# A four-layer attention network on one core: block-end copies, a norm in three parts, gates and a bias moved

## The chip, the cores and the metric

The kernel runs on one core of a Trainium2 chip. A core has five engines that work side by side, each through its own list of instructions: TensorE (PE, matrix products; its weight loads are listed as PEld), VectorE (DVE), ScalarE (ACT), GpSimd (POOL) and SyncE (SP), which here only issues transfers. The products land in PSUM[...]; DVE and ACT carry them from there to SBUF. The metric is the time of the whole program on the device in microseconds (us); lower is better.

## The reference, cut to what matters

Input is `x`, two images of 64 x 64 positions with 128 channels. Four residual layers follow each other: attention with relative positions, a triangle product, attention with an expert layer, attention with an expert layer. The change touches the first two.

```python
def _gn(v, G=32, eps=1e-5):                      # group norm over the positions of one image
    g = v.reshape(B_, H_, W_, G, C_ // G)
    return ((g - mean(g)) / sqrt(var(g) + eps)).reshape(v.shape)

# layer 0: x = x + L0(_gn(x))
scores = einsum('bnqd,bnkd->bnqk', q, k) * scale + pos     # 2 images, 4 heads, 4096 x 4096
out = einsum('bnqk,bnkd->bnqd', softmax(scores), v)

# layer 1: x = x + L1(_gn(x))
xn = layer_norm(x, norm_a, norm_b)
left = (xn @ Wl + bl) * sigmoid(xn @ Wlg + blg)
right = (xn @ Wr + br) * sigmoid(xn @ Wrg + brg)
out_gate = sigmoid(xn @ Wog + bog)
out = einsum('bkjd,bkid->bijd', left, right) / n           # the triangle product
out = layer_norm(out, on_a, on_b) * out_gate
return out @ Wo + bo
```

## The kernel before

All of `x` stays in SBUF as 64 blocks of 128 positions x 128 channels. Everything is float32.

**Layer 0** (`l0_bounded`) works in eight units: image, pair of heads, half of the queries. A unit has four blocks of 512 queries (`qb`), a block 32 steps of 128 keys (`k`). In a step PE makes the scores of two heads (L588, `l0sc`), ACT takes the exponential (L596, `l0es`), DVE multiplies with the position factor `ew` (L597), and the product with the values is made two steps later by `values()` (L546, `l0o`). `waiting` holds the two steps in between. When a block's last key has been multiplied, `values()` copies the sums out of PSUM, half on ACT (L555), half on DVE (L556), into `os`; `l0o` has one buffer, so the next block's first product waits for both copies. Then `l0_finish` adds the two halves of `os` (L705), transposes, divides and adds to `x`. In the text the multiply of a step stands before the call of `values()`.

Between the steps the text hands out small pieces of other work: `piece()` the next unit's queries, keys and position factors (`l0_prepare`) and `l0_finish`; `more()`, every fourth step, group statistics and, once image 0 is through (from half of layer 0 on), layer 1's norm of image 0 (`l1_first`).

**Layer 1** starts with the second image's norm, which can't start before layer 0 ends. `l1_rows` makes the group statistics and spreads them to rows (`gb`, L150), then for all eight groups of four blocks the group norm (L157, L158: DVE, 128 x 512), then for all 32 blocks the row statistics (L165, L166), then one chain for the reciprocal roots (`rstd`, L93 to L102, with a square root on ACT, L95), then 32 normalizations, even blocks on DVE (L169), odd ones on ACT (L428). `l1_turn` then transposes a group of four blocks on PE (L443) and brings it back through ACT with `norm_a` and `norm_b` (L444). `gates` makes the output gate of a group: a product (L897) and an eviction by ACT (L900); image 0's gates stand before image 1's norm, image 1's behind each turn. The sigmoid of the gates stands in the text among the projections (L947).

The projections (L925) take columns of `xT` with stride 64, so they need both images whole. 32 pairs follow each other: products on PE, bias on DVE (L933), sigmoid on ACT (L937), two multiplies on POOL (L939). Then comes the triangle product (L960), brought out by ACT (L967) into `tri`; beside it the text adds the bias `bo` to `x` on DVE (L974, sixteen times). `bo` itself is loaded at the start of layer 1 with the weights, by SP. Behind the triangle product SP loads the table for layer 2 (`kept`, L1040, 1792 KB), and DVE makes the statistics of `tri`.

What sets the order: the text gives each instruction its dependencies and its rank, and a planner fixes each engine's list when the program is built. An engine's list is not the text's order. In the trace, for example, the adds of L974 run from 2201.5 us on, before the projections, and the gates' sigmoids of L947 start at 2189.2 us.

Of the kernel before, what the change touches and what calls it, by code (L numbers as in the profile page):

```python
# [39 lines left out]
class Net:  # L40
# [356 lines left out]
    def l1_first(self, ps, xT, st, gb, na, nb):  # L397

        nc = self.nc
        for _ in self.l1_rows(ps, xT, 0, st, gb):  # L400
            yield
        for g in range(NC // 4):
            self.l1_turn(ps, xT, 0, g, na, nb)
            yield

    def l1_rows(self, ps, xT, b, st, gb):


        nc = self.nc
        self.group_rows(ps, gb, self.group_stats(ps, st, b))  # L410
        yield
        y = xT.rearrange("p (n c) -> p n c", c=C)
        mv = self.small.tile([P, NC, 2], F32, tag="l2mv", name=f"l1mv{b}", bufs=2)
        for g in range(NC // 4):
            blk = slice(4 * g, 4 * g + 4)
            self.group_norm(y[:, blk, :], b, g, gb)
            yield
        for n in range(0, NC, 2):
            self.row_stats(mv[:, n : n + 2, :], y[:, n : n + 2, :], f"l1{b}_{n}")
            yield  # L420
        r = self.small.tile([P, NC], F32, tag="l2r", name=f"l1r{b}", bufs=2)
        self.rstd(r, mv[:, :, 1], 1e-5, NC)
        m = self.small.tile([P, NC], F32, tag="l1m", name=f"l1m{b}", bufs=1)
        nc.vector.scalar_tensor_tensor(m, mv[:, :, 0], -1.0, r, ALU.mult, ALU.mult)
        yield
        for n in range(NC):
            if n % 2:
                nc.scalar.activation(  # L428
                    y[:, n, :], y[:, n, :], AF.Identity, bias=m[:, n : n + 1], scale=r[:, n : n + 1]
                )  # L430
            else:
                self.normalize(y[:, n, :], y[:, n, :], mv, r, n)
            if n % 4 == 3:
                yield

    def l1_turn(self, ps, xT, b, g, na, nb):
# [27 lines left out]
    def l0_bounded(self, xT, w, pe, gst, na, nb):  # L464
# [13 lines left out]
        nc, tc = self.nc, self.tc  # L478
        H2 = L // 2
        with (  # L480
# [91 lines left out]
            for i, unit in enumerate(units):  # L572
                ready(unit)
                qa, ew = made[unit]
                b, pair, half = unit
                ka = kas[pair]
                if i + 1 < len(units):
                    side.append(self.l0_prepare(ap, ps, units[i + 1], xT, wqk, pe, kas, made))
                for qb in range(4):
                    qs = slice(qb * 512, (qb + 1) * 512)  # L580
                    t = f"{b}_{pair}_{half}_{qb}"
                    for k in range(NC):
                        sc = ps.tile([P, 2, 512], F32, tag="sc", name=f"l0sc{t}_{k}")
                        for h in range(2):
                            rows = slice(64 * h, 64 * h + 64)
                            for c in range(2):
                                k0 = k * P + 64 * c
                                nc.tensor.matmul(  # L588
                                    sc[64 * c : 64 * c + 64, h, :],
                                    lhsT=ka[rows, k0 : k0 + 64],  # L590
                                    rhs=qa[rows, k // (NC // 2), qs],
                                    start=True,
                                    stop=True,
                                )
                        es = ap.tile([P, 2, 512], F32, tag="es", name=f"l0es{t}_{k}", bufs=3)
                        nc.scalar.activation(es, sc, AF.Exp)  # L596
                        nc.vector.tensor_tensor(es, es, ew[:, :, qs], ALU.mult)  # L597
                        if len(waiting) == 2:
                            values()
                        waiting.append((unit, qb, k, es))  # L600
                        if k % 2:
                            piece()
                        elif k % 4 == 2:
                            more()
# [236 lines left out]
    def layer1(self, xT, gst, na, nb, xp, kp):  # L841
# [3 lines left out]
        nc, tc, ins = self.nc, self.tc, self.ins  # L845
        GN = 16
        with ExitStack() as st:
            wp = st.enter_context(tc.tile_pool(reuse_waits="tile", name="l1w", bufs=1))
            sp = st.enter_context(tc.tile_pool(reuse_waits="tile", name="l1n", bufs=2))
            big = st.enter_context(tc.tile_pool(reuse_waits="tile", name="l1b", bufs=1))  # L850
            names = ("l", "r", "lg", "rg", "og")
            wcat = wp.tile([P, 5 * C], F32, tag="wcat", name="wcat")
            bcat = wp.tile([P, 4 * C], F32, tag="bcat", name="bcat")
            for i, n in enumerate(names):
                nc.sync.dma_start(out=wcat[:, i * C : (i + 1) * C], in_=ins[f"L1_conv_W{n}"])
                if i < 4:
# [10 lines left out]
                )  # L867
            )
            wo = self.load(wp, "wo", [P, C], ins["L1_conv_Wo"])
            bo = self.load(wp, "bo", [P, C], row_bcast(ins["L1_conv_bo"], C))  # L870

            def stats(src, tag):

# [14 lines left out]
                else:  # L888
                    self.normalize(rows, rows, mv, r, i)

            gate = big.tile([P, B, L], F32, tag="gate", name="l1gate")
            with tc.tile_pool(reuse_waits="tile", name="l1p", bufs=6, space=PSUM) as ps:

                def gates(b, g):
                    blk = slice(g * 512, (g + 1) * 512)
                    pg = ps.tile([P, 512], F32, tag="misc", name=f"l1pg{b}_{g}")
                    nc.tensor.matmul(  # L897
                        pg, lhsT=wcat[:, 4 * C :], rhs=xT[:, b, blk], start=True, stop=True
                    )
                    nc.scalar.activation(gate[:, b, blk], pg, AF.Identity, bias=bog)  # L900

                self.group_block(ps, gst[:, 1], 1, NC // 4 - 1)
                gb = sp.tile([P, 2 * C], F32, tag="gb", name="l1gb", bufs=1)
                rows = self.l1_rows(ps, xT[:, 1, :], 1, gst[:, 1], gb)
                next(rows)
                for g in range(NC // 4):
                    gates(0, g)
                for _ in rows:
                    pass
                for g in range(NC // 4):  # L910
                    self.l1_turn(ps, xT[:, 1, :], 1, g, na, nb)
                    gates(1, g)
            xnT = xT.rearrange("p b l -> p (b l)")
            gate = gate.rearrange("p b l -> p (b l)")


            lr = kp.tile([P, 2, C, S], F32, tag="k", name="lr")
            with (
                tc.tile_pool(reuse_waits="tile", name="l1t", bufs=3) as tp,
                tc.tile_pool(reuse_waits="tile", name="l1q", bufs=3, space=PSUM) as ps,  # L920
            ):
                for j in range(0, S, 2):
                    p1 = ps.tile([P, 2, 4 * C], F32, tag="lr", name=f"l1p1_{j}")
                    for k in range(2):
                        nc.tensor.matmul(  # L925
                            p1[:, k, :],
                            lhsT=xnT[:, j + k :: S],
                            rhs=wcat[:, : 4 * C],
                            start=True,
                            stop=True,  # L930
                        )
# [1279 lines left out]
```

## Time and profile before

| | |
|---|---|
| runs, median of 3 | 4906.94 us (4905.28 to 4908.01) |
| the profiled execution | 4914.85 us, its span 4913.0 us |
| TensorE's mean granted clock | 0.954 of full |
| busy: PE, DVE, ACT, POOL | 4556.6 (93%), 2937.1 (60%), 2666.8 (54%), 922.1 (19%) us |

The stretches of layer 1 in the same execution, busy microseconds of each engine in each stretch:

| stretch, us from the start | PE | DVE | ACT | POOL | clock | what runs |
|---|---|---|---|---|---|---|
| 2173 to 2183 | 6.01 | 3.57 | 3.57 | 0.00 | 0.50 | group statistics |
| 2183 to 2193 | 9.27 | 9.55 | 6.50 | 0.00 | 0.80 | group norm, gates of image 0 |
| 2193 to 2202 | 0.00 | 9.00 | 4.80 | 0.00 | 0.73 | row statistics |
| 2202 to 2208 | 0.00 | 6.00 | 0.23 | 0.00 | 0.50 | reciprocal roots, adds of `bo` |
| 2208 to 2242 | 21.82 | 9.54 | 21.28 | 0.00 | 0.56 | normalization, turns, gates of image 1 |
| 2242 to 2300 | 54.95 | 39.19 | 21.92 | 45.38 | 1.00 | projections |
| 2300 to 2319 | 17.82 | 0.00 | 14.96 | 0.47 | 0.83 | triangle product |
| 2319 to 2360 | 22.46 | 34.23 | 26.68 | 18.16 | 0.68 | norm of the product, gate |

In a line of a timeline the first number is the start in us, the second the time that it takes; then engine, line, operation, what is written and read, shapes, and how many were merged. In square brackets stands how long the engine had been idle and what ended that. In a line of the costliest groups, behind the bar, stand the busy time and the mean of one in ns, and behind the second bar the engine's idle time ahead of them and what ended most of it. A matrix product of the text is listed as two instructions.

### The profile page before, as it was taken

Reading aid. Unit: us, or ns where it says so; the run is one execution under the profiler, and the core shown is the slowest. Engines: PE = TensorE matmul, PEld = TensorE weight load, DVE = VectorE, ACT = ScalarE, POOL = GpSimd, SP = SyncE. Lnnn points to the kernel's source line nnn. Section 1 sums busy time; section 2 is a strip of 40 time slices with the busy share of each in tenths; the row PEclk is TensorE's granted clock in tenths of the full one; section 3 lists DMA queues with packets and bytes.
Section 4 is the critical chain, followed back from the end, with each engine's and each line's share of the span. In section 5 each row is a group of like instructions: output and inputs, shape, how many; then the busy total and the mean of one; then the engine's idle time right before and its main releaser. Section 6 shows DMA issues by size and latency. Waiting matters only on the chain.

```text
span 4913.0 us, 78463 instructions
## 1 busy us (share of the span) xinstructions
PE 4556.6 (93%) x33360; PEld 1785.9 (36%) x33360; DVE 2937.1 (60%) x4864; ACT 2666.8 (54%) x3100; POOL 922.1 (19%) x832
## 2 busy tenths in 40 slices
PE   6999999999999999977789999999967999999999
PEld 4333333333233333325322223222225444444443
DVE  4676767676766767774755666555553444454447
ACT  4555555555656555555567766676631443333335
POOL 1000000000000000003355555555520000000008
PEclk7999999999999999988899999999978999999999
DMA  1000000000000000000000000000034000000001
GB/s 46 10 1 10 1 10 1 10 1 10 1 1 10 1 12 1 1 8 16 8 1 1 1 1 1 1 1 1 1 106 176 0 1 1 0 1 0 0 1 35
DMA packets 43355, 60.30 MB, mean 12 GB/s; under 512 B 4496, under 2 KB 25200, under 8 KB 41840
## 3 DMA queue, kind: packets, MB, share of 16 engines
q1 hardware_dynamic: 41696, 54.34, 3.5%
q8 instruction: 265, 4.34, 0.4%
q10 hardware_dynamic: 1296, 0.82, 0.1%
q14 instruction: 98, 0.80, 0.1%
HBM read 42.57 MB, written 4.19 MB: 10 GB/s over the span
## 4 chain that ended last, share of the span: by engine, by line
PE 38%; DVE 6%; ACT 3%; POOL 3%; issue 2%; DMA 0%; POOLq 0%; DVEq 0%; ACTq 0%
PE scl L2048 9%; PE oTl L2008 9%; PE l2sc L1422 5%; PE l2pos L1180 4%; PE l2av L1468 3%; PE f3ex L2142 2%; DVE l2es L1442 2%; POOL l2es L1445 2%; ACT l2es L1453 1%; ACT l2es L1433 1%; PE l2po L1388 1%; DVE l2a L169 0%; PE f3fpb L1938 0%; PE l2pu L1180 0%; PE f2pp L1613 0%
## 5 line engine op out<-in xcount | busy, mean ns | idle before, releaser
L597 DVE TENSOR_TENSOR l0es<-l0es,l0ew 128x1024 f32<-128x1024 f32 x1024 | 1251.9, 1227 | 603.3 <-ACT l0es L596 603.3
L596 ACT ACTIVATE l0es<-l0sc 128x1024 f32<-128x1024 f32 x1024 | 1043.5, 1024 | 721.9 <-PE l0sc L588 712.3
L546 PE MATMUL l0o<-l0es,l0v 64*33 64x512 f32 x8192 | 1069.8, 592 | 51.7 <-DVE l0os L556 46.4
L588 PE MATMUL l0sc<-l0qa,ka 64*64 64x512 f32 x8192 | 1081.9, 597 | 4.7 <-ACT l0es L596 4.6
L1453 ACT ACTIVATE l2es<-l2es 128x1024 f32<-128x1024 f32 (+3 forms) x576 | 560.0, 984 | 274.7 <-POOL l2es L1445 266.8
L1445 POOL TENSOR_TENSOR l2es<-l2es 128x1024 f32<-128x1024 f32 (+3 forms) x352 | 581.4, 1662 | 489.4 <-DVE l2es L1442 417.3
L2016 DVE TENSOR_TENSOR accl<-accl,esl 128x1024 f32<-128x1024 f32 x240 | 293.8, 1224 | 430.4 <-ACT esl L2059 426.5
L1442 DVE TENSOR_SCALAR l2es<-l2sc 128x1024 f32<-128x1024 f32 (+3 forms) x320 | 338.6, 1058 | 316.4 <-PE l2sc L1422 313.6
L2059 ACT ACTIVATE esl<-scl 128x1024 f32<-128x1024 f32 x240 | 245.8, 1024 | 472.5 <-PE scl L2048 446.7
L546 PEld LDWEIGHTS l0o<-l0es,l0v 64*33 64x33 f32 x8192 | 257.9, 108 | 659.4 <-issue 564.3
L588 PEld LDWEIGHTS l0sc<-l0qa,ka 64*64 64x64 f32 x8192 | 294.8, 133 | 547.4 <-issue 480.9
L2048 PE MATMUL scl<-l3qT,l3kT 128*128 128x512 f32 x1024 | 486.3, 595 | 0.0
L1422 PE MATMUL l2sc<-l2q,kept 32*128 32x512 f32 (+3 forms) x2304 | 391.7, 628 | 83.3 <-ACT l2es L1433 63.3
L2008 PE MATMUL oTl<-esl,l3v 128*128 128x512 f32 x960 | 450.9, 592 | 0.0
L722 POOL TENSOR_TENSOR x<-x,l0y 128x256 f32<-128x256 f32 x32 | 23.4, 732 | 2074.4 <-DVE l0y L717 1945.9
L1468 PE MATMUL l2av<-l2es,kept 128*32 128x512 f32 (+3 forms) x2304 | 314.8, 594 | 0.0
L1180 PE MATMUL l2pos<-kept 128*32 128x512 f32 x2416 | 297.3, 600 | 0.0
L2008 PEld LDWEIGHTS oTl<-esl,l3v 128*128 128x128 f32 x960 | 181.8, 190 | 225.8 <-issue 222.9
L2048 PEld LDWEIGHTS scl<-l3qT,l3kT 128*128 128x128 f32 x1024 | 186.9, 190 | 199.8 <-issue 186.0
L1433 ACT ACTIVATE l2es<-l2sc 128x1024 f32<-128x1024 f32 x224 | 226.4, 1010 | 48.6 <-PE l2sc L1422 47.1
L1422 PEld LDWEIGHTS l2sc<-l2q,kept 32*128 32x128 f32 x2304 | 117.1, 189 | 327.3 <-ACT l2es L1433 165.3
L1979 POOL TENSOR_TENSOR bothl<-accl 128x512 f32<-128x512 f32 x16 | 20.2, 1265 | 799.2 <-DVE accl L2016 799.2
(733 smaller groups left out, 3882.0 us busy)
## 6 DMA issues: line engine op xcount, KB each, us to landing
f2w<-in_L_ffn_weight_dram SPq DMA_DIRECT2D x32, 1024.0 KB, 13.5
l0ew<-l0ew SPq DMA_DIRECT2D x16, 512.0 KB, 5.1
x<-in_x_dram SPq DMA_DIRECT2D x8, 512.0 KB, 8.9
out_dram<-x SPq DMA_DIRECT2D x16, 256.0 KB, 2.3
kept<-in_L_attn_pos_rev_dram SPq DMA_DIRECT2D x1, 1792.0 KB
ew<-in_L_ffn_expert_w_dram SPq DMA_DIRECT2D x1, 512.0 KB, 4.0
kept<-in_L_attn_pos_rev_dram SPq DMA_DIRECT2D x1, 256.0 KB, 3.1
f2b<-in_L_ffn_weight_dram ACTq DMA_DIRECT2D x2, 128.0 KB, 2.5
```

Of the source, the lines that this page charges most:

```text
L546: nc.tensor.matmul(o[64 * h : 64 * h + HD + 1, r, :], lhsT=v1[rows, k, 2 * pair + h, :], rhs=es[rows, h, :], start=(k == 0), stop=(k == NC ...
L588: nc.tensor.matmul(sc[64 * c : 64 * c + 64, h, :], lhsT=ka[rows, k0 : k0 + 64], rhs=qa[rows, k // (NC // 2), qs], start=True, stop=True,)
L596: nc.scalar.activation(es, sc, AF.Exp)
L597: nc.vector.tensor_tensor(es, es, ew[:, :, qs], ALU.mult)
L1180: nc.tensor.matmul(out[part], lhsT=lhsT[:, part], rhs=rhs, start=start, stop=stop)
L1422: nc.tensor.matmul(sc[:, h2, off:], lhsT=kT[hs, k * P : (k + 1) * P], rhs=q[hs, off:], start=True, stop=True,)
L1442: nc.vector.tensor_scalar(es[:, :, lo:], sc[:, :, lo:], root, None, ALU.mult)
L1445: nc.gpsimd.tensor_tensor(part, part, part, ALU.mult)
L1453: nc.scalar.activation(es[:, :, off:], es[:, :, off:], AF.Silu)
L1468: nc.tensor.matmul(avs[i][hs, off:], lhsT=v[:, k, hs], rhs=es[h // 2][:, h % 2, off:], start=(k == 0), stop=last,)
L2008: nc.tensor.matmul(oT, lhsT=vs[b][:, k, :], rhs=es[:, i, :], start=(k == 0), stop=(k == NC - 1),)
L2048: nc.tensor.matmul(sc[:, i, :], lhsT=kTs[b][:, k * P : (k + 1) * P], rhs=qT[:, qb * 512 : (qb + 1) * 512], start=True, stop=True,)
```

## The change

Layer 0: `values()` is called before the multiply with `ew`, so that the copies of a block's end stand before the step's multiply in the text.

Layer 1: `l1_rows` makes the row statistics of a group right behind its group norm, and takes a list of groups. For the second image it is called for three groups, three and two, each with its own reciprocal roots, and followed by the turns of these groups; all its normalizations go to ACT. The gates of image 0 stand before that, in a PSUM buffer of their own (one bank); the gates of image 1 stand between the projections, one in every second pair of the first half. `bo` is loaded ahead of the triangle product into a buffer of that stage.

```diff
-        for _ in self.l1_rows(ps, xT, 0, st, gb):
+        self.group_rows(ps, gb, self.group_stats(ps, st, 0))
+        yield
+        for _ in self.l1_rows(xT, 0, gb, range(NC // 4)):
             yield
...
+    def l1_rows(self, xT, b, gb, blocks, pool=None):
+        nc = self.nc
+        y = xT.rearrange("p (n c) -> p n c", c=C)
+        lo, n = 4 * blocks[0], 4 * len(blocks)
+        mv = self.small.tile([P, NC, 2], F32, tag="l2mv", name=f"l1mv{b}_{lo}", bufs=2)
+        for g in blocks:
+            self.group_norm(y[:, 4 * g : 4 * g + 4, :], b, g, gb)
+            yield
+            for i in range(0, 4, 2):
+                at = 4 * g + i
+                self.row_stats(
+                    mv[:, at - lo : at - lo + 2, :], y[:, at : at + 2, :], f"l1{b}_{at}"
+                )
+                yield
+        r = self.small.tile([P, NC], F32, tag="l2r", name=f"l1r{b}_{lo}", bufs=2)
+        self.rstd(r[:, :n], mv[:, :n, 1], 1e-5, n, pool)
+        m = self.small.tile([P, NC], F32, tag="l1m", name=f"l1m{b}_{lo}", bufs=2)
+        nc.vector.scalar_tensor_tensor(m[:, :n], mv[:, :n, 0], -1.0, r[:, :n], ALU.mult, ALU.mult)
         yield
+        for i in range(n):
+            rows = y[:, lo + i, :]
+            if b == 0 and i % 2 == 0:
+                self.normalize(rows, rows, mv, r, i)
+            else:
                 nc.scalar.activation(
+                    rows, rows, AF.Identity, bias=m[:, i : i + 1], scale=r[:, i : i + 1]
                 )
...
                         nc.scalar.activation(es, sc, AF.Exp)
-                        nc.vector.tensor_tensor(es, es, ew[:, :, qs], ALU.mult)
                         if len(waiting) == 2:
                             values()
+                        nc.vector.tensor_tensor(es, es, ew[:, :, qs], ALU.mult)
                         waiting.append((unit, qb, k, es))
...
-            bo = self.load(wp, "bo", [P, C], row_bcast(ins["L1_conv_bo"], C))
...
-            with tc.tile_pool(reuse_waits="tile", name="l1p", bufs=6, space=PSUM) as ps:
-                def gates(b, g):
+            def output_gate(ps, g):
+                blk = slice(g * 512, (g + 1) * 512)
+                pg = ps.tile([P, 512], F32, tag="pg", name=f"l1pg{g}", bufs=1)
+                nc.tensor.matmul(pg, lhsT=wcat[:, 4 * C :], rhs=xnT[:, blk], start=True, stop=True)
+                nc.scalar.activation(gate[:, blk], pg, AF.Identity, bias=bog)
+            with tc.tile_pool(reuse_waits="tile", name="l1p", bufs=5, space=PSUM) as ps:
                 self.group_block(ps, gst[:, 1], 1, NC // 4 - 1)
                 gb = sp.tile([P, 2 * C], F32, tag="gb", name="l1gb", bufs=1)
-                rows = self.l1_rows(ps, xT[:, 1, :], 1, gst[:, 1], gb)
-                next(rows)
+                self.group_rows(ps, gb, self.group_stats(ps, gst[:, 1], 1))
                 for g in range(NC // 4):
-                    gates(0, g)
-                for _ in rows:
-                    pass
-                for g in range(NC // 4):
-                    self.l1_turn(ps, xT[:, 1, :], 1, g, na, nb)
-                    gates(1, g)
+                    output_gate(ps, g)
+                for blocks in (range(3), range(3, 6), range(6, 8)):
+                    for _ in self.l1_rows(xT[:, 1, :], 1, gb, blocks, sp):
+                        pass
+                    for g in blocks:
+                        self.l1_turn(ps, xT[:, 1, :], 1, g, na, nb)
...
                 for j in range(0, S, 2):
+                    if j % 4 == 2 and j < S // 2:
+                        output_gate(ps, (L + 128 * (j - 2)) // 512)
                     p1 = ps.tile([P, 2, 4 * C], F32, tag="lr", name=f"l1p1_{j}")
...
                 tri = xp.tile([P, S, C], F32, tag="xT", name="tri")
+                bo = up.tile([P, C], F32, tag="bo", name="bo", bufs=1)
+                nc.sync.dma_start(out=bo, in_=row_bcast(ins["L1_conv_bo"], C))
                 for d8 in range(C // 8):
```

More of the change, by code (lines that the diff above doesn't have):

```diff
@@ L404, in l1_first @@
             yield
-    def l1_rows(self, ps, xT, b, st, gb):
+    def l1_rows(self, xT, b, gb, blocks, pool=None):
         nc = self.nc
-        self.group_rows(ps, gb, self.group_stats(ps, st, b))
-        yield
-        y = xT.rearrange("p (n c) -> p n c", c=C)
-        mv = self.small.tile([P, NC, 2], F32, tag="l2mv", name=f"l1mv{b}", bufs=2)
-        for g in range(NC // 4):
[L415 to L427, printed above, removed]
+        y = xT.rearrange("p (n c) -> p n c", c=C)
[14 more added lines that the diff above has]
+        nc.vector.scalar_tensor_tensor(m[:, :n], mv[:, :n, 0], -1.0, r[:, :n], ALU.mult, ALU.mult)
+        yield
+        for i in range(n):
[3 more added lines that the diff above has]
+            else:
@@ L428, in l1_rows @@
                 nc.scalar.activation(
-                    y[:, n, :], y[:, n, :], AF.Identity, bias=m[:, n : n + 1], scale=r[:, n : n + 1]
+                    rows, rows, AF.Identity, bias=m[:, i : i + 1], scale=r[:, i : i + 1]
                 )
-            else:
-                self.normalize(y[:, n, :], y[:, n, :], mv, r, n)
-            if n % 4 == 3:
+            if i % 4 == 3:
                 yield
@@ L889, in norm @@
                     self.normalize(rows, rows, mv, r, i)
-            gate = big.tile([P, B, L], F32, tag="gate", name="l1gate")
-            with tc.tile_pool(reuse_waits="tile", name="l1p", bufs=6, space=PSUM) as ps:
-                def gates(b, g):
[L895 to L900, printed above, removed]
+            gate = big.tile([P, B * L], F32, tag="gate", name="l1gate")
+            xnT = xT.rearrange("p b l -> p (b l)")
+            def output_gate(ps, g):
[4 more added lines that the diff above has]
+            with tc.tile_pool(reuse_waits="tile", name="l1p", bufs=5, space=PSUM) as ps:
                 self.group_block(ps, gst[:, 1], 1, NC // 4 - 1)
                 gb = sp.tile([P, 2 * C], F32, tag="gb", name="l1gb", bufs=1)
-                rows = self.l1_rows(ps, xT[:, 1, :], 1, gst[:, 1], gb)
-                next(rows)
+                self.group_rows(ps, gb, self.group_stats(ps, gst[:, 1], 1))
                 for g in range(NC // 4):
-                    gates(0, g)
-                for _ in rows:
-                    pass
-                for g in range(NC // 4):
-                    self.l1_turn(ps, xT[:, 1, :], 1, g, na, nb)
-                    gates(1, g)
-            xnT = xT.rearrange("p b l -> p (b l)")
-            gate = gate.rearrange("p b l -> p (b l)")
+                    output_gate(ps, g)
[4 more added lines that the diff above has]
+                        self.l1_turn(ps, xT[:, 1, :], 1, g, na, nb)
             lr = kp.tile([P, 2, C, S], F32, tag="k", name="lr")
```

## The prediction

> **What bounds the kernel now.** I read the page first (busy times, costliest groups), then the tile view of `l0os`, then timelines: a block end, a block end with other DVE work beside it, and the start of layer 1.
>
> ```profile
> L597 DVE TENSOR_TENSOR l0es<-l0es,l0ew 128x1024 f32<-128x1024 f32 x1024 | 1251.9, 1227 | 603.3 <-ACT l0es L596 603.3
> L596 ACT ACTIVATE l0es<-l0sc 128x1024 f32<-128x1024 f32 x1024 | 1043.5, 1024 | 721.9 <-PE l0sc L588 712.3
> L546 PE MATMUL l0o<-l0es,l0v 64*33 64x512 f32 x8192 | 1069.8, 592 | 51.7 <-DVE l0os L556 46.4
> ```
>
> DVE waits for ACT and ACT for PE, so TensorE sets the pace of layer 0; its largest named wait there is 46.4 us for the copy on L556. The tile view says how often:
>
> ```profile
> L556 DVE COPY l0os<-l0o x32: 681/684/693, 192.3 to 2168.3; 97x512 f32<-97x512 f32 x32
> ...
>   PE l0o L546: 46.4, 30
> ```
>
> Thirty block ends at 1.55 us each. One of them in order of time:
>
> ```profile
> 1021.21 1.04 PE L546 MATMUL l0o<-l0es,l0v 64*33 64x512 f32 x8
> ...
> 1022.51 1.23 DVE L597 TENSOR_TENSOR l0es<-l0es,l0ew 128x1024 f32<-128x1024 f32 x1 [0.47 <-ACT l0es L596]
> ...
> 1023.76 0.69 DVE L556 COPY l0os<-l0o 97x512 f32<-97x512 f32 x1
> ...
> 1024.51 1.06 PE L546 MATMUL l0o<-l0es,l0v 64*33 64x512 f32 x8 [1.41 <-DVE l0os L556]
> ```
>
> The block's last product ends at 1022.25; DVE takes the step's multiply first, then the copy, and PE stands 1.41 us. Next, the same place where the norm of image 0 runs beside:
>
> ```profile
> 1235.00 1.21 DVE L597 TENSOR_TENSOR l0es<-l0es,l0ew 128x1024 f32<-128x1024 f32 x1
> 1236.13 0.24 DVE L166 BATCH_NORM_AGGREGATE l1mv<-stl 128x2 f32<-128x6 f32 x2
> 1236.40 0.69 DVE L556 COPY l0os<-l0o 97x512 f32<-97x512 f32 x1
> ```
>
> Here two `bn_aggr` of the norm stand between multiply and copy, though the text has them dozens of steps after it. And layer 1:
>
> ```profile
> 2201.50 0.66 DVE L974 TENSOR_TENSOR x<-x,bo 128x512 f32<-128x512 f32 x1
> ...
> 2208.45 6.26 ACT L428 ACTIVATE xT<-xT,l1m,l1r 128x128 f32<-128x128 f32 x16 [5.27 <-DVE l1m L424]
> ...
> 2226.92 2.08 PE L897 MATMUL l1pg<-xT,wcat 128*128 128x512 f32 x2 [0.87 <-ACT xT L444]
> ...
> 2229.04 0.69 ACT L900 ACTIVATE l1gate<-l1pg,bog 128x512 f32<-128x512 f32 x1 [2.17 <-PE l1pg L897]
> ...
> 2241.85 28.49 PE L925 MATMUL l1p<-wcat,xT 128*128 128x512 f32 x66
> ```
>
> From the group's rows (`gb`, done 2183.1) to the first projection (2241.85) are 58.7 us in which no engine is full: DVE alone to 2208, then the chain turn, gate, eviction, with 3.8 us a block.
>
> **What the Trainium skill says.** "TensorE: Matmul & The Clock Gate", section "Part 1: The HAM clock gate": TensorE runs at half its clock until it has been busy for about 3.4 us. The trace agrees: L897 takes 2.07 us per two passes at 2215 to 2236 and 1.12 us at 2238. The same page, section "Architectural detail", says that VectorE and ScalarE are strict first-in, first-out. The trace shows nothing against it; so the order fixed at build counts, not who is ready on the chip. "ScalarE: Activation LUTs", section "What ACT_TABLE_LOAD costs", puts a load at 1283 ns; the trace has 1.28 us.
>
> **Part 1, layer 0.** One line moves: `values()` before the multiply. Only DVE's order can change (PE and ACT keep theirs), and only at the 32 block ends, where `values()` ends in a DVE copy. If the copy does go ahead: it starts at the last product's end, 1022.37 (as ACT's half does now), ends 1023.05, PE goes on at 1023.12 instead of 1024.51. The multiply ends 0.5 us later, at 1024.28, and its product comes due at 1024.84: hidden. Gain per block 1.39 us, over 31 waits 43 us; where PE stood 2.03 us (seven ends, with half clock after) up to 1 us more each. Taken: 44.
>
> But does it? The trace shows that the text's order is not the engine's: `x<-x,bo` of L974 runs at 2201, before the projections that the text has ahead of it; the os add (L705), two steps later in the text, runs before the next multiply. So instructions are placed when they are expected to be ready. Then the text decides only between two that are ready together. How long the planner thinks a step takes can be read off: between two multiplies at 1219.05 and 1226.74 it put four or five 0.6 us norm operations into DVE's idle time, 3.5 to 4.1 us per step with the multiply, where the chip takes 1.72. Twice the chip's step means that it counts the two halves of a product one after the other: some 1.7 us for `values` after the scores end, against about 1.1 us for the Exp. The multiply is then ready about 0.6 us before the copy, and DVE takes it first whatever the text says. The fence at 1235 agrees: even behind the multiply the copy was not ready, or later-text `bn_aggr` would not stand before it. So I take **0 us** for part 1, and keep 44 as the other end. A loss is excluded by the 0.5 us worked out above.
>
> The norm of image 0 inside layer 0 keeps its instructions (group norm and row statistics now alternate per block). They fill DVE as before: 0, plus or minus 3.
>
> **Part 2, layer 1 before the projections.** Removed from this stretch: the 16 adds of `bo` (ten of them, 6.2 us, at 2201 to 2208 between statistics and rstd), eight gates of image 1 (PE 2.07, ACT 0.69 each), the barrier of one rstd over all 32 rows. Added: two more rstd chains, all 32 normalizations on ACT rather than 16.
>
> DVE: 16 group-norm operations x 0.60 = 9.6, 32 row statistics x 0.26 = 8.4, three rstd chains of 2.0 (1244.04 to 1245.98 in layer 0), partly filled by the next part: some 21 us, done about 2205. ACT becomes the stretch's bound: 8 evictions of gates x 0.69 = 5.5; 4 sigmoids x 1.06 = 4.2; 32 normalizations x 0.39 = 12.5; 8 turns x 0.76 = 6.1; 3 square roots 0.6; table loads, as sigmoid and square root alternate, two before, two to six now, taken four, 5.1. Sum 34 us. It starts with the first gate at 2185.5, so it ends about 2219.5. From below: two loads and gates that run fast, 2212. From above: the gates of image 0 now share one PSUM bank, matmul and eviction in turn, at half clock 1.7 + 0.69 + 0.3 = 2.7 us each, 21.6 us, and part one's turns behind them on PE: 2228. Taken 2219: gain 22.9 us.
>
> **Part 3, gates in the projections.** 2242 to 2300 is PE's (54.95 busy of 58 us): 8 gates x 2 passes x 0.43 = +6.9 us. ACT has room there (0.63 of 1.72 us a pair), POOL too (1.43). The cold start of TensorE is now paid there: about 4 us at half clock, +2.
>
> **Part 4, `bo` late.** Its issue (0.43 us on SP) leaves the start of layer 1. The 16 adds (0.63 each, 10.1 us) go to the triangle product, where DVE idles 21.1 us before 2319.4 while PE and ACT work. The load must wait for the projections' SBUF if it lands there; 2 us of landing plus 10.1 fit: 0. Without that cover they would cost up to 10.1.
>
> Sum: 22.9 - 6.9 - 2 = 14 us. The profiled execution took 4914.85 us (span 4913.0), 8 above the median 4906.94; I subtract from the median: **4893 us**. The own range of this case is 4886 (ACT done 2212) to 4902 (2228).
>
> **Rivals.**
> - *The copy does go ahead.* For it: the wait is real and the move exactly right for the chip's times. Against: the order argument above. 4906.9 - 44 - 14 = 4849.
> - *Layer 1 gives back what it saves.* Single bank, half clock and table loads bring the first projection to 2228 or later; 14 - 9 or less: about 4903, no change that can be told. For it: the ping-pong at 2215 to 2238 never got fast.
> - *Slower: `bo` behind the table on SP.* The 1792 KB load of `kept` is issued at 2318.5 and takes 23.6 us. If `bo` sits behind it in SP's queue while its adds stand before the statistics on DVE, these start about 2352 rather than 2319.4: +33 - 14 = +19, 4926. It decides from a landing after 2309. Against: `bo` comes first in the text and waits for less.
>
> **How the numbers follow.** Chances: forecast 0.60, copy ahead 0.20, given back 0.13, slower 0.07. About 0.2% (9.8 us) is what a measurement of this kernel tells from no change. The forecast case lies below 4897.1 in about three quarters of its chance (0.45), else within: faster 0.45 + 0.20 = 0.65 and a little of the third case, 0.68; same 0.23; slower 0.09. The range 4842 to 4904 takes in the copy case, the forecast and most of the third.
>
> **What would show it.** In the changed profile: L556's wait on PE near 46 us means part 1 did nothing, near 0 that I misread the order. First L925 matmul about 36 us after `gb`, not 59. ACT nearly without gaps there, with three square roots. Eight L897-like gates among the projections, which then last about 67 us. L974 beside the triangle product (L960), and the statistics of `tri` right behind its last eviction (L967). Wrong if the order at the block ends changed, or if PE waits for the gate bank throughout.

## The result and the profile after

| | before | after |
|---|---|---|
| median | 4907.81 us, 20 runs (4898.31 to 4918.73) | 4897.74 us, 20 runs (4891.29 to 4901.57) |
| the profiled execution | 4914.85 us, span 4913.0 us | 4895.63 us, span 4893.8 us |
| mean granted clock in it | 0.954 | 0.957 |

The ratio of after to before is 0.9977, with a 95% interval of 0.997 to 0.9984: about 10 us faster, where 14 were forecast. A run is the shorter, the higher its mean granted clock, so small differences are compared at equal clock as well: at 0.957 the kernel before took 4906.9 us on average (22 runs of all its sets) and the changed kernel 4896.8 (11 runs of after and of e9 below), at 0.955 4911.4 (19) and 4901.3 (8), 10.1 less both times. All "before" medians below were measured beside the run they are compared with; they lie between 4906.69 and 4910.47.

Layer 0 first: the costliest groups of the profile after. The code has moved by four lines: L603 is the multiply, L600 the exponential, L550 the product with the values.

```profile
L603 DVE TENSOR_TENSOR l0es<-l0es,l0ew 128x1024 f32<-128x1024 f32 x1024 | 1251.8, 1227 | 601.2 <-ACT l0es L600 601.2
L600 ACT ACTIVATE l0es<-l0sc 128x1024 f32<-128x1024 f32 x1024 | 1042.5, 1023 | 718.0 <-PE l0sc L592 715.0
L550 PE MATMUL l0o<-l0es,l0v 64*33 64x512 f32 x8192 | 1068.1, 591 | 52.0 <-DVE l0os L560 46.3
```

The last number of the last line was 46.4 before. One block end of after in order of time, from the timeline:

```profile
946.90 2.36 DVE L603 TENSOR_TENSOR l0es<-l0es,l0ew 128x1024 f32<-128x1024 f32 x2 [0.35 <-ACT l0es L600]
...
947.67 0.59 ACT L559 COPY l0os<-l0o 97x512 f32<-97x512 f32 x1
...
949.29 0.69 DVE L560 COPY l0os<-l0o 97x512 f32<-97x512 f32 x1
...
950.04 1.06 PE L550 MATMUL l0o<-l0es,l0v 64*33 64x512 f32 x8 [2.03 <-DVE l0os L560]
```

DVE still takes two multiplies without a break (`x2`) and the copy behind them, although the text now has the copy ahead of the second; PE stands 2.03 us. The copy could have started about 0.4 us before the second multiply did (ACT's half, which waits for the same product, starts at 947.67). Nothing has changed here.

Layer 1 is where the time went. Busy time of the engines in two stretches, from the group's rows to the first projection and to the last one, first of before, then of after; columns are the stretch, its length, PE, PEld, DVE, ACT, POOL busy (instructions), the granted clock, the DMA share and GB/s:

```profile
2183.10:2241.90 58.80, 30.88 (x70) 14.55 (x71) 33.99 (x132) 32.81 (x51) 0.00 (x0) 0.62 0.00 1
2241.90:2297.00 55.10, 55.05 (x129) 37.44 (x127) 37.96 (x31) 21.04 (x33) 42.95 (x60) 1.00 0.00 0
```

```profile
2177.50:2218.40 40.90, 27.06 (x53) 10.26 (x53) 21.17 (x110) 33.04 (x60) 0.00 (x0) 0.54 0.00 1
2218.40:2282.60 64.20, 64.17 (x144) 41.15 (x144) 38.31 (x34) 31.45 (x47) 42.91 (x60) 0.97 0.00 1
```

To a hundredth, they were 58.75 and 55.10 us long before, and 40.97 and 64.21 after. The first lost 17.8 us, the second grew by 9.1 with the eight gates in it and a start at half clock: 8.7 us net. ACT's busy time in the first hardly changed in sum (32.81 and 33.04 us): what went is its idle time. What it still waited for stands in the timeline of after:

```profile
2180.57 2.08 PE L900 MATMUL l1pg<-xT,wcat 128*128 128x512 f32 x2 [0.78 <-ACT l1gate L901]
2182.68 0.69 ACT L901 ACTIVATE l1gate<-l1pg,bog 128x512 f32<-128x512 f32 x1 [2.17 <-PE l1pg L900]
2183.39 1.28 ACT L950 ACT_TABLE_LOAD   x1
2183.42 2.08 PE L900 MATMUL l1pg<-xT,wcat 128*128 128x512 f32 x2 [0.78 <-ACT l1gate L901]
...
2194.28 0.69 ACT L901 ACTIVATE l1gate<-l1pg,bog 128x512 f32<-128x512 f32 x1 [1.01 <-PE l1pg L900]
2194.86 1.25 ACT L434 ACTIVATE xT<-xT,l1m,l1r 128x128 f32<-128x128 f32 x3
...
2197.13 0.69 ACT L901 ACTIVATE l1gate<-l1pg,bog 128x512 f32<-128x512 f32 x1 [1.02 <-PE l1pg L900]
```

Product and eviction of a gate take turns in their one PSUM buffer (a bank, 128 x 512 float32), a gate every 2.85 us. ACT's list has the evictions between the normalizations of part one (L434, in threes), so these wait as well. The list of waits of this stretch sums it up (total, times, longest, in us):

```profile
ACT l1gate L901 <- PE l1pg L900: 10.2, 6, 4.8
```

The longest is the first, begun ahead of the stretch; the other five make 5.4 us inside it.

The bias, in the timeline of after: the load is issued at 2284.47, ahead of the table (2302.99), the adds run beside the triangle product, and the statistics of `tri` come when its last eviction is done.

```profile
2287.30 9.72 DVE L979 TENSOR_TENSOR x<-x,bo 128x512 f32<-128x512 f32 x16 [3.30 <-DMA bo<-in_L_conv_bo_dram]
...
2304.01 0.49 DVE L165 BATCH_NORM_STATS2 stl1o<-tri 128x6 f32<-128x128 f32 x2 [6.99 <-ACT tri L972]
```

### The profile page after: what moved, and what is told of

Same layout as the page of the kernel before. It is cut to its first block, busy times and chain, and to the rows that moved or that the text cites. A ratio compares the mean times of both kernels' runs of the same rounds, so it can differ in the third digit from the quotient of the medians.

```text
span 4893.8 us, 78484 instructions
## 1 busy us (share of the span) xinstructions
PE 4551.0 (93%) x33360; PEld 1780.2 (36%) x33360; DVE 2934.4 (60%) x4862; ACT 2675.0 (55%) x3122; POOL 920.8 (19%) x832
## 4 chain that ended last, share of the span: by engine, by line
PE 38%; DVE 6%; ACT 3%; POOL 3%; issue 2%; DMA 0%; POOLq 0%; DVEq 0%; ACTq 0%
PE scl L2053 9%; PE oTl L2013 9%; PE l2pos L1185 5%; PE l2sc L1427 5%; PE l2av L1473 3%; PE f3ex L2147 2%; DVE l2es L1447 2%; POOL l2es L1450 2%; ACT l2es L1458 1%; ACT l2es L1438 1%; PE l2po L1393 1%; DVE l2a L169 0%; PE f3fpb L1943 0%; PE l2pu L1185 0%; DVE f2xn L169 0%
## 5 line engine op out<-in xcount | busy, mean ns | idle before, releaser
L603 DVE TENSOR_TENSOR l0es<-l0es,l0ew 128x1024 f32<-128x1024 f32 x1024 | 1251.8, 1227 | 601.2 <-ACT l0es L600 601.2
L600 ACT ACTIVATE l0es<-l0sc 128x1024 f32<-128x1024 f32 x1024 | 1042.5, 1023 | 718.0 <-PE l0sc L592 715.0
L550 PE MATMUL l0o<-l0es,l0v 64*33 64x512 f32 x8192 | 1068.1, 591 | 52.0 <-DVE l0os L560 46.3
L550 PEld LDWEIGHTS l0o<-l0es,l0v 64*33 64x33 f32 x8192 | 257.7, 108 | 658.3 <-issue 562.1
```

Source lines behind the costliest of these rows:

```text
L550: nc.tensor.matmul(o[64 * h : 64 * h + HD + 1, r, :], lhsT=v1[rows, k, 2 * pair + h, :], rhs=es[rows, h, :], start=(k == 0), stop=(k == NC ...
```

## The experiments

Stretches of the main runs, in us from each trace: `layer 0` from the first score to the group's rows of image 1, `norm` from there to the first projection, `proj` the projections, `tri` to the end of the triangle product, `rest` from layer 1's output product to the end (the 49 to 50 us between the last two, alike in all, are left out).

```
                     layer 0    norm   proj    tri     rest
before               2085.79   58.75  55.10  21.39  2544.57
e1_move_alone        2083.88   57.53  55.10  20.14  2543.24
after                2081.12   40.97  64.21  20.27  2540.82
e9 (after again)     2085.84   40.89  64.17  20.27  2540.42
e2_copy_forced       2056.66   40.05  64.97  21.24  2537.44
e5_two_sums          2042.66   40.48  63.84  20.27  2540.28
e3_gate_banks        2084.02   36.05  64.44  18.73  2543.42
e4_norm_split        2080.31   33.91  64.69  21.12  2544.00
e7_gates_behind      2080.77   51.30  55.64  20.20  2543.30
e6_bo_early          2085.53   40.92  64.32  18.72  2543.62
e10 (e6 again)       2081.71   42.53  64.81  21.17  2544.15
e12_bo_late_alone    2083.55   56.14  55.10  20.28  2544.09
e8_together          2042.76   34.04  64.68  21.11  2540.35
e11_late_sigmoids    2041.30   29.39  64.76  21.14  2540.72
```

**Layer 0: the moved line alone** (on the kernel before).

```diff
-                        nc.vector.tensor_tensor(es, es, ew[:, :, qs], ALU.mult)
                         if len(waiting) == 2:
                             values()
+                        nc.vector.tensor_tensor(es, es, ew[:, :, qs], ALU.mult)
```

> The kernel before with the one moved line of layer 0 and nothing of layer 1. Theory (each engine's list is fixed by when an instruction is expected to be ready, and the copy is expected after the multiply): the lists stay as they were, PE's wait for the block-end copy on DVE stays at 46 us, the time stays within 0.2% of before (a ratio of 0.998 to 1.002). Rival (the move does put the copies ahead, and the 46 us of the changed kernel have another cause, such as ACT's half of the copy): DVE's copy starts about 1.3 us earlier in each block against the product's end.

Measured: 4909.01 us (12 runs) beside 4910.47; ratio 0.9998, 0.9989 to 1.0007. PE's wait is 46.4 us at 30 block ends, and the lists that the build fixed for all five engines are, entry for entry, those of before. The move does nothing in this kernel; its layer 0, 1.9 us from that of before, shows what drifts between executions of one list. By the clock records of the traces the drift goes with the granted clock: TensorE was at half clock for 41 us of layer 0 in before and in e9, for 36 in e1 and for 30 in after, and layer 0 took 2085.8, 2083.9 and 2081.1 us.

**The copy put ahead by force** (on the kernel after): the step's multiply is queued behind DVE's copy at a block end.

```diff
-                    nc.vector.tensor_copy(os[rows, 1, :], o[rows, 1, :])
+                    end = nc.vector.tensor_copy(os[rows, 1, :], o[rows, 1, :])
...
-                        if len(waiting) == 2:
-                            values()
-                        nc.vector.tensor_tensor(es, es, ew[:, :, qs], ALU.mult)
+                        end = values() if len(waiting) == 2 else None
+                        with tc.issue_after(end.ins) if end is not None else nullcontext():
+                            nc.vector.tensor_tensor(es, es, ew[:, :, qs], ALU.mult)
```

> The changed kernel with an explicit order: the multiply of a block-end step is queued behind that block's DVE copy. Theory: the wait is real and only the order was missing, so PE's wait for the copy falls from 46 us to under 10, the multiply is hidden, and the time falls by another 35 to 48 us against the changed kernel, to about 4850 to 4863. Rival (the delayed multiply is late for its own product, or PE waits next for ACT's half of the copy): the named wait falls but another takes its place, and less than 15 us come off.

Measured: 4868.62 us (5 runs), ratio 0.9913, 0.99 to 0.9927: 29 us off after between medians, but 25 at the clock of 0.958 that four of the five runs had (4868.9 us against 4893.5 in eight runs of after and e9), and 24.5 less layer 0 than in after's trace. That is under the 35 to 48 expected, and over the rival's 15. The same block end in its timeline, and two lines from the view of the tile `l0os` (who waited, us, times):

```profile
937.11 0.59 ACT L559 COPY l0os<-l0o 97x512 f32<-97x512 f32 x1
...
937.74 0.69 DVE L560 COPY l0os<-l0o 97x512 f32<-97x512 f32 x1 [0.17 <-ACT l0os L559]
...
938.48 1.06 PE L550 MATMUL l0o<-l0es,l0v 64*33 64x512 f32 x8 [1.03 <-DVE l0os L560]
```

```profile
  DVE l0os L560: 26.1, 31
  PE l0o L550: 24.9, 30
```

PE's wait falls from 46.3 to 24.9 us, not to zero: DVE's copy now stands until ACT's copy has ended, at 31 of the 32 ends; the second part of the rival, a wait for ACT's half, is what happened. The two read different halves of one PSUM tile `o`, and the build orders them one after the other. The price of the rival in the forecast had the copy start when the product ends, as ACT's half does; ACT's 0.6 us were missing in it.

**The sums in two PSUM tiles** (on the kernel above).

```diff
-            o = ps.tile([P, 2, 512], F32, tag="o", name="l0o", bufs=1)
-            nc.vector.memset(o, 0.0)
+            o = [ps.tile([P, 512], F32, tag=f"o{r}", name=f"l0o{r}", bufs=1) for r in range(2)]
+            for r in range(2):
+                nc.vector.memset(o[r], 0.0)
...
-                    nc.scalar.copy(os[rows, 0, :], o[rows, 0, :])
-                    end = nc.vector.tensor_copy(os[rows, 1, :], o[rows, 1, :])
+                    nc.scalar.copy(os[rows, 0, :], o[0][rows])
+                    end = nc.vector.tensor_copy(os[rows, 1, :], o[1][rows])
```

> As e2_copy_forced, with the block's sums in two PSUM tiles of one bank each instead of one tile of two banks. Theory (in e2 DVE's copy still waits for ACT's half because both read one tile; 26 us of DVE idle stand before it): the copy starts about 0.6 us earlier in 31 blocks, PE's wait falls from 25 us to under 8, 15 to 20 us come off e2, to about 4849 to 4854. Rival (the wait for ACT hides another for PE's last product, or the multiply becomes late): under 5 us.

Measured: 4856.66 us (4 runs), ratio 0.9899, 0.9883 to 0.9916: 12 us less again between medians, under the 15 to 20 expected, and 16 at equal clock (at 0.957: 4856.0 us in three runs, 40.8 under the changed kernel). From its timeline and its tile view:

```profile
930.17 0.59 ACT L560 COPY l0os<-l0o 97x512 f32<-97x512 f32 x1
...
930.66 0.69 DVE L561 COPY l0os<-l0o 97x512 f32<-97x512 f32 x1
930.82 1.22 PE L551 MATMUL l0o<-l0es,l0v 64*33 64x512 f32 x5 [0.30 <-ACT l0os L560]
```

```profile
  PE l0o L551: 3.1, 7
```

DVE's copy starts before ACT's has ended, here and at 30 more of the 32 ends, at most of them within 0.1 us of ACT's start, and PE goes on after 0.30 us: each half is now free for itself. Together 41 us under after (4897.74 - 4856.66), near the 44 that the forecast gave to "the copy does go ahead"; it takes two edits that the change doesn't have.

**Layer 1: three banks for image 0's gates** (on after).

```diff
-            def output_gate(ps, g):
+            def output_gate(ps, g, bufs=1):
...
-                pg = ps.tile([P, 512], F32, tag="pg", name=f"l1pg{g}", bufs=1)
+                pg = ps.tile([P, 512], F32, tag="pg", name=f"l1pg{g}", bufs=bufs)
...
-            with tc.tile_pool(reuse_waits="tile", name="l1p", bufs=5, space=PSUM) as ps:
+            with tc.tile_pool(reuse_waits="tile", name="l1p", bufs=3, space=PSUM) as ps:
...
-                    output_gate(ps, g)
+                    output_gate(ps, g, 3)
```

> The changed kernel with three PSUM banks for image 0's gates instead of one (three for the turns instead of five). Theory (one bank makes gate product and eviction take turns at half clock, ACT waits for them between the normalizations of part one): from the group's rows to the first projection 33 to 37 us instead of 41, 4 to 8 us off the time. Rival (ACT's 33 us of work and its order bound the stretch): 0 to 2 us.

Measured: 4894.71 us (6 runs), ratio 0.9968, 0.9956 to 0.998. Its stretch, and part one of the norm in its timeline:

```profile
2179.40:2215.40 36.00, 22.28 (x53) 9.88 (x53) 21.34 (x110) 32.72 (x60) 0.00 (x0) 0.64 0.00 1
```

```profile
2186.86 2.84 PE L900 MATMUL l1pg<-xT,wcat 128*128 128x512 f32 x6 [1.15 <-ACT l1gate L901]
...
2193.66 4.71 ACT L434 ACTIVATE xT<-xT,l1m,l1r 128x128 f32<-128x128 f32 x12
```

ACT's work is the same (32.72 against 33.04 us), but the twelve normalizations of part one follow without a gate between them, and the first projection comes 36.05 us after the group's rows, 4.9 earlier than in after. Of the 5.4 us of waits 0.7 are left, and it is the 36 us of the forecast. The time follows only in part: the median is 3 us under after's, where 4 to 8 were expected, and at equal clock nothing is clear (4895.5 against 4896.8 us at 0.957, 4894.0 against 4893.5 at 0.958); `rest` is 2.6 us longer. In 2180 to 2190 the granted clock is 0.86 here and 0.50 in after: six passes take 2.84 us, where two take 2.08 in after. So the edit changed the bank and the clock together, and what each alone costs isn't separated. That the clock has a part shows in e6 and e10 below, two executions of one kernel with one bank: TensorE was at half clock for 34 us of this stretch in e6 and for all of it in e10, ACT waited 4.2 and 5.9 us for gates, and the first projection came after 40.92 and 42.53 us.

**Even normalizations on DVE again** (on after).

```diff
-            if b == 0 and i % 2 == 0:
+            if i % 2 == 0:
                 self.normalize(rows, rows, mv, r, i)
```

> The changed kernel with image 1's even blocks normalized on DVE again (16 of 32). Theory (ACT bounds the stretch before the projections): 16 x 0.39 = 6.2 us leave ACT, the first projection comes 4 to 6 us earlier. Rival (the gates' single bank and the late square roots set it, ACT waits anyway): 0 to 2 us, the freed time shows as ACT idle.

Measured: the stretch is 33.91 us, 7.1 less, with ACT busy 26.93 of it; so ACT's list does bound this stretch.

```profile
2176.20:2210.20 34.00, 23.31 (x55) 10.06 (x54) 25.19 (x127) 26.93 (x44) 0.00 (x0) 0.60 0.00 1
```

The median is 4897.18 us (8 runs; ratio 0.9972, 0.9962 to 0.9983), hardly under after's. Two of the eight runs had a clock of 0.953; two at 0.957 took 4891.5 us, 5 under the changed kernel, and three at 0.956 4897.4, 2 under it. In the table its `rest` is 3.2 us longer, of which more below.

**Image 1's gates behind the turns again** (on after).

```diff
                     for g in blocks:
                         self.l1_turn(ps, xT[:, 1, :], 1, g, na, nb)
+                        output_gate(ps, NC // 4 + g)
...
-                    if j % 4 == 2 and j < S // 2:
-                        output_gate(ps, (L + 128 * (j - 2)) // 512)
```

> The changed kernel with the gates of image 1 behind each part's turns instead of between the projections. Theory: the projections shrink from 64 to about 56 us, the stretch before grows by 8 evictions (5.5 us of ACT) and half-clock products (8 x 2.07 us of PE, partly beside the normalizations), 6 to 14 us; net 0 to +6. Rival (the products of the gates are hidden beside the normalizations and the move to the projections gained nothing): net -4 or less.

Measured: 4898.42 us (20 runs), ratio 0.9985, 0.9978 to 0.9992. Norm +10.3, projections -8.6: 1.7 us net. The median is 0.7 us above after's. The gates cost nearly the same in either place.

**The bias loaded early again** (on after), twice, the second time beside the changed kernel itself.

```diff
+            bo = self.load(wp, "bo", [P, C], row_bcast(ins["L1_conv_bo"], C))
...
-                bo = up.tile([P, C], F32, tag="bo", name="bo", bufs=1)
-                nc.sync.dma_start(out=bo, in_=row_bcast(ins["L1_conv_bo"], C))
```

> The changed kernel with the bias loaded at the start of layer 1 again. Theory (the adds of the bias run as soon as the bias is there, between the statistics and the roots): L974's 16 adds run before the projections, and the stretch from the group's rows to the first projection grows by 3 to 6 us. Rival (ACT bounds that stretch now and DVE has 20 us to spare): under 1.5 us.

> The changed kernel once more, as the neighbour of the next run on the same chip. Expected 4893 to 4902; its stretches from the group's rows to the triangle product's end within 2 us of the first profile's 125.4.

> The kernel of e6_bo_early beside the changed kernel. There its median stood 6 us above that of the changed kernel while the stretch was no longer (123.96 against 125.44). If the bias's place costs nothing both agree within 3 us; if it costs something outside that stretch, the 6 us come back and show in a later stretch.

Measured: e6 4903.6 us (12 runs; ratio 0.9993, 0.9985 to 1.0002), e9 4896.18 us (13 runs; 0.9975, 0.9967 to 0.9984), e10 4903.69 us (13 runs; 0.999, 0.9982 to 0.9998). The difference comes back: 7.5 us between neighbours on one chip. The adds run before the projections again (from 2202.35 us on in e6), but DVE has room there. ACT has one table load more in the stretch in both (busy 34.1 us against 33.1), yet the first projection is not later in e6 (40.92), where ACT waited 1.2 us less for gates than in after; the 1.6 us in e10 are those of the clock named above, for both have the same lists. What both traces share is a `rest` 2.8 to 3.7 us longer, though PE, DVE, ACT and POOL do the same there in the same order. Sorted by the granted clock of each run, the early load is some 3 us slower at equal clock (0.955: 4904.3 against 4901.3 us; 0.957: 4899.5 against 4896.8), and its runs have the lower clocks more often. So of the 6 to 7.5 us between medians some 3 are left at equal clock; whether the early load also brings the lower clocks isn't shown.

**The late bias alone** (on the kernel before; the same edit the other way round).

> The kernel before with the late load of the bias alone. Theory from the pairs with and without it (6 and 7.5 us between medians): the ten adds leave DVE between the row statistics and the reciprocal roots (6.2 us at 2202 to 2208), the first projection comes up to 6 us earlier, and the median falls by 4 to 8 us against before. Rival (the bias's place costs nothing by itself, as the forecast's part 4 had it, and the pairs differ by their granted clocks alone): within 3 us of before.

Measured: 4902.75 us (22 runs) beside 4906.69; ratio 0.999, 0.9984 to 0.9997: 4 us, and 4.7 at equal clock (4902.2 us in nine runs at 0.957 against 4906.9). From its timeline:

```profile
2198.77 0.33 DVE L97 RECIPROCAL rs_r<-rs_s 128x32 f32<-128x32 f32 x1
...
2200.26 6.26 ACT L428 ACTIVATE xT<-xT,l1m,l1r 128x128 f32<-128x128 f32 x16 [1.96 <-DVE l1m L424]
```

The normalization starts 21.5 us after the group's rows (2178.74 here) instead of 25.4 (2208.45 - 2183.10): 3.8 us, of which 2.6 reach the first projection. Ten adds of 0.62 us had stood there, but between them ran the chain of the roots, which itself takes 2.6 us now (L93 at 2197.45 to L424 at 2200.03). The fall of the median is at the lower end of what was expected, and the first projection comes by less than half of the 6 us.

**Together**: two sums, three gate banks and even normalizations on DVE.

> The changed kernel with the forced copy, two sum tiles, three banks for image 0's gates and image 1's even blocks normalized on DVE. If the gains add: e5's and another 5 to 9 us from the stretch before the projections, about 4841 to 4849. If ACT waits for something else there: no more than e5.

Measured: 4850.48 us (4 runs), ratio 0.9885, 0.9868 to 0.9901: 6 us under e5, just outside what was expected if the gains add. They don't: the stretch takes 34.04 us, no less than the 33.91 of e4 with its one bank. ACT has seven table loads there now, of 1.28 us each, where e4 and after have five, because each of the three square roots stands between two sigmoids.

**The sigmoids late** (on that kernel), queued behind the last square root of the norm.

```diff
-        nc.scalar.activation(s, v, AF.Sqrt)
+        self.root = nc.scalar.activation(s, v, AF.Sqrt)
...
+            root = self.root
...
-                        nc.scalar.activation(part, part, AF.Sigmoid)
+                        with tc.issue_after(root.ins):
+                            nc.scalar.activation(part, part, AF.Sigmoid)
```

> As e8_together, with the sigmoids of the gates queued behind the last square root of the norm. Theory (ACT bounds the stretch; table loads and the sigmoids are part of it): two to three loads of 1.28 us and up to 4 sigmoids of 1.06 leave; the stretch from the group's rows to the first projection falls from 34 to 27-31, and 3 to 6 us off e8_together's 4850.5. Rival: another wait takes their place, and under 1.5 us comes off.

Measured: 4846.36 us (4 runs), ratio 0.9872, 0.9857 to 0.9888. The stretch in both kernels, e8 above and e11 below:

```profile
2139.10:2173.20 34.10, 19.98 (x54) 9.84 (x53) 25.59 (x127) 30.35 (x47) 0.00 (x0) 0.65 0.00 1
```

```profile
2138.70:2168.20 29.50, 17.82 (x55) 9.50 (x54) 25.49 (x127) 20.08 (x38) 0.00 (x0) 0.67 0.00 1
```

Six of seven table loads, where two to three were expected, and three of four sigmoids leave the stretch: ACT's busy time falls by 10.3 us and the length by 4.65. DVE, busy 25.49 of 29.50 us, has taken over as the bound: ACT now stands 4.4 us for DVE's factors (`l1m`). This version is 64 us under before and 50 under the change (against e9).

## Why the prediction was nearly right

In the order of its steps; the measured column is after against before in the traces, with e9 as a second trace where it differs.

| step | forecast | measured |
|---|---|---|
| part 1, copy ahead of the multiply | 0 | 0 (46.3 us against 46.4; e1: 0.9998) |
| part 2, stretch to the first projection | -22.9 us | -17.8 us |
| part 3, gates and cold start in the projections | +8.9 us | +9.1 us |
| part 4, bias beside the triangle product | 0 | `tri` -1.1 us |
| layer 0 apart from that | 0 ± 3 | -4.7 us, in e9 0.0 |
| behind layer 1 | none named | -3.8 us, in e9 -4.2 |
| median | -14 us | -10.1 us; e9: -13.9 |

**Part 1 was right**, as to what happens: the move in the text changes no engine's list (e1). The reason given, that the planner counts the halves of a product one after the other and so finds the multiply ready first, fits but was not tested; shown is only that the text's order is not what decides here. Its other end, 44 us, was the wait as a whole and had DVE's copy start with ACT's; in one tile it comes behind it, and forcing the order alone gave 25 us at equal clock. With two tiles the 41 us came.

**Part 2 is the mis-sized term.** The bound was named rightly: ACT's work was summed to 34 us and measured 33.0, with five table loads where four were taken. But the sum was taken as ACT's time without gaps. The forecast had the ping-pong of the gates in one bank as its upper end (2.7 us a gate; 2.85 measured) and then took the sum without it, although PE and ACT wait for each other there: five waits of ACT for a gate, 5.4 us. With 1.0 us less work than summed they make nearly all of the 5.1 us between -22.9 and -17.8, and e3, which only gives the gates three banks, puts the first projection where the forecast had it. The rival "layer 1 gives back" had the right mechanism at 9 us or more; half of that came. Of the three square roots the last two came together, behind part one's turns in ACT's list (2204.66); DVE stood 4.0 us for them, but ACT did not, so it cost the path nothing that a trace shows.

**Part 3 was right in size.** e7 adds what the forecast didn't say: the gates behind the turns cost as much, so of this part only 1.7 us in the trace is gain.

**Part 4**: the cover held as described, and the slower rival (the bias behind the table) fell with the order of the two loads, 18 us apart. The -1.1 us of `tri` isn't the bias's: e1 has 20.14 us with the bias early, and e6 and e10, one kernel, have 18.72 and 21.17. What the forecast missed is that the place of the bias is worth something by itself: 4 us on the kernel before, where its adds stood on the path between statistics and roots, and some 3 us of the changed kernel's 10 at equal clock (6 to 7.5 between medians). One table load on ACT, 1.28 us, is all of it that the stretch before the projections shows there; the rest stays open.

**Luck** is that e9's 13.9 us come so near to 14. At equal clock e9 and after stand alike, 10.1 us under before. The steps that the forecast summed give 8.7 us in the trace (-17.8 and +9.1); what part 2 lacks is covered in part by the 4 us behind layer 1, which no step of the forecast named.

**Left open**: the 3 to 4 us in `rest`. It takes 2540.3 to 2540.8 us in after, e9, e5, e8 and e11, 2537.4 in e2, 2543.2 to 2544.6 in all others, and no order of PE, DVE, ACT or POOL differs there. The clock differs: in the first 4 us from layer 1's output product it was 0.64 to 0.65 in before, after, e9 and e12 and 0.50 in all others, whose products are 1.1 to 1.6 us behind those of after within 10 us. But this doesn't decide the end: before and e12 start like after and end 3 us later, e5 starts late and ends like after. Nor is it shown that `rest` belongs to the kernel, for only two were profiled twice: after and e9 run within 0.4 us of each other throughout, e6 and e10 lie up to 2.8 us apart on the way and end 0.5 apart. No run tested what sets it.

## What to carry to other kernels

Where a program fixes the order at build, moving a line of text is a request; look in the next profile at the two instructions on their engine before giving it a price, and if the order matters, state it as a dependency. When an engine's work in a stretch is summed up, add the waits of each buffer that it shares in turn with another engine: with a single bank, product and eviction add up and do not overlap (2.85 us a gate here). When the bound is taken away, ask at once which engine is next: here ACT's 10 us less bought 4.65.

## What was not expected of the hardware

- Two engines that read different halves of one PSUM tile went one after the other (26.1 us at 31 block ends in e2), and side by side once each half was a tile. The Trainium skill ("PSUM — Partial Sum Buffer", section "PSUM bank collisions raise a hardware error") has two engines on different banks run clean; the halves are 2 KB a partition each, one bank, and e5, where the two copies run at the same time at 31 of 32 ends, agrees. So the order in e2 went with the tile and not with the banks; that the build guards the tile as a whole is the likely reason.
- TensorE stayed at half clock while it worked in turn with ACT, with idle times of only 0.78 to 0.87 us: 0.50 in 2180 to 2190 of after. The same skill ("TensorE: Matmul & The Clock Gate", section "A second HAM failure mode: psum-queue depth-cycling") tells of a kernel that swings between half and full clock as it cycles through PSUM; here one bank kept it at half, and three banks brought 0.86 in the same ten microseconds.
- Layer 0 of one and the same kernel took 2081.1 us in one profiled execution and 2085.8 in another, with 30 and 41 us of it at half clock, so a difference below 5 us there says nothing about an edit.
